# GNN layer with residual norm on one core: rows of x held in runs by partition, and an earlier order of the first loads

## The chip, the cores and the metric

One core of a Trainium2 chip runs the whole program. The metric is the device time of one execution in microseconds. It is 1736.49 us before the change, the median of three runs (1736.48 to 1737.98).

## The reference

`x` has 12500 nodes of 128 values, and there are 400000 edges, sorted by their destination. Each edge has one of two types.

```python
Xs = X[src]
m_data = Xs @ W_data.T + b_data
m_ctrl = Xs @ W_control.T + b_control
msg = jnp.where((edge_types == 0)[:, None], m_data, m_ctrl)
agg = jax.ops.segment_sum(msg, dst, num_segments=X.shape[0])
out = agg + (X @ W_self.T + b_self)
x = _layernorm(x + jax.nn.relu(out), axis=-1)
```

The sum over edges is done on rows of x, and the weights are applied once to the sums of each type.

## The kernel before

The 3125 chunks of 128 edges form 25 groups of 125 chunks (`NG`, `GC`). A group has four or five sets; there are 107 in all (`pairs`). A group's chunks are treated in two ways.

Most chunks of a set (20, "e") are *picked*: x lies in SBUF as `x3`, each fp32 value split into three bf16 parts, and a 0/1 matrix (`pick`, 128 x 100 cells x 32 ranks) lets TensorE choose the rows (`rows`, L899, tile `got`). ScalarE evicts the result (`emsg`, L907), and TensorE adds it into `sums` with a second 0/1 matrix over the nodes (`esel`, the node columns, made on VectorE by `select`). For this every edge of the set is given a cell and a rank in its cell: `give_slots` (L566) makes `O`, counts with `ltri` on TensorE, and forms `rank`, `rm`, `rv`; `put` and `spread` bring that through a small tile `there` in DRAM to all partitions as `pick`. A cell belongs to a *place*: x3 has 98 places (`NBLK`) of up to 128 rows. The index of a row is cut into its lane (partition) and its place in `prep(...).then` (L492).

The other chunks ("p") and the few edges without a slot (`spare_rows`, L862) are *gathered*: GpSimd's indirect DMA reads rows of `rows3`, a copy of x3 in DRAM with 768 bytes a row (`fetch`, L788). Gathered chunks enter from the third set on (`LAG = 2`). A first gather has to wait until rows3 is whole.

Sums are added to a running tile `acc` at places that are read from the chip's own table `place_i` (`place_of`, L772; `accumulate`, L778): VectorE's sequencer loads the place into a register for each addition. `finish` multiplies by the weights and normalises.

Before the first set, `split_x` (L268) brings x from DRAM in pieces of 14 blocks. In a block, row `b*128 + p` lies on partition p, so one piece's load consists of 14 runs of 512 bytes on each partition, issued by ScalarE's queue. `split` takes the three parts out of each piece with three ScalarE instructions (L286, L288) and two on VectorE (L290, L293), and `store` writes the piece to rows3 from SP's queue, in runs of 768 bytes. Four tiles `xt` hold pieces in flight. Meanwhile group 0 is prepared (`prep(0)`), the slots of sets 0 and 1 are given, and the small transfers run: `load(0)`, `load_first` (ten transfers of 25 numbers), weights and biases (nine). The order of instructions on each engine follows the code, but a scheduler may move an instruction within it; `tc.issue_after(i)` holds instructions until i is issued in that order. Each queue works strictly in its order.

Of the kernel before, what the change touches and what calls it, by code (L numbers as in the profile page):

```python
# [8 lines left out]
FP = mybir.dt.float32  # L9
# [35 lines left out]
NBLK = -(-N // P)  # L45
NQ = 25
# [4 lines left out]
AHEAD = 14  # L51
FAR = -(-PW // DPC)
# [102 lines left out]
def row_tables(nc, keep, tmp):  # L155
# [21 lines left out]
    nc.vector.tensor_single_scalar(pick_first, pick_first_cols(nc, tmp, col), 0.0, op=OP.is_equal)  # L177
# [16 lines left out]
def pick_first_cols(nc, tmp, col):  # L194

    cols = tmp.tile([P, 3, GC], FP, name="cols")
# [6 lines left out]
    return cols  # L203


def short_path(ctx, tc, const, ident, eps, wT, brow, bad, x, src, dst, etype, ws, bs, out):
# [52 lines left out]
    load_first("e")  # L259
    load_first("p")  # L260

    early, pro = ExitStack(), ExitStack()
    parted = []
# [4 lines left out]
    def split_x(pool):  # L268

        tiles, units = {}, []  # L270
        pieces = [(b, min(step, NBLK - b), P) for b in range(0, NBLK, step)]
        b, m, _ = pieces.pop()
        pieces += [(b, m - 1, P), (b + m - 1, 1, N - (NBLK - 1) * P)]

        def at(t, b, m, rows):
            return t[b * P:b * P + (m - 1) * P + rows, :].rearrange("(k p) d -> p k d", p=rows)

        def fetch(b, m, rows):
            t = tiles[b] = pool.tile([P, step, D], FP, name="xt")[:rows, :m, :]
            nc.scalar.dma_start(out=t, in_=at(x, b, m, rows))  # L280

        def split(b, m, rows):
            t = tiles.pop(b)
            part = x3[:rows, b:b + m]
            byte = t.bitcast(U8).rearrange("p k (d b) -> p k d b", b=4)
            nc.scalar.copy(part[:, :, 0, :], t.bitcast(BF).rearrange("p k (d b) -> p k d b", b=2)[:, :, :, 1])  # L286
            for j in range(2):
                nc.scalar.activation(part[:, :, 2 - j, :], byte[:, :, :, j], AF.Copy, scale=2.0 ** (8 * j - 23))  # L288
            power = pool.tile([P, step, D], BF, name="power", bufs=2)[:rows, :m, :]
            nc.vector.tensor_single_scalar(  # L290
                power.bitcast(I16), part[:, :, 0, :].bitcast(I16), -128, op=OP.bitwise_and
            )
            parted.append(nc.vector.tensor_tensor(  # L293
                part[:, :, 1:, :], part[:, :, 1:, :],
                power.rearrange("p k (j d) -> p k j d", j=1).to_broadcast([rows, m, 2, D]), op=OP.mult,
            ))

        def store():
            for b, m, rows in pieces:
                nc.sync.dma_start(  # L300
                    out=at(rows3, b, m, rows), in_=x3[:rows, b:b + m].rearrange("p k j d -> p k (j d)")
                )

        ahead = 4
# [9 lines left out]
        return units, store  # L314

    split_units, store_rows = split_x(pro.enter_context(tc.tile_pool(name="pro", bufs=4)))
# [4 lines left out]
    for i, (w, b) in enumerate(zip(ws, bs)):  # L321
        nc.sync.dma_start(out=wn[:, i, :], in_=w)
        row = b.rearrange("(o d) -> o d", o=1)
        nc.sync.dma_start(out=brow[:, i, :], in_=row)
        at = (0, CAP, 2)[i]
        nc.sync.dma_start(out=bias[at:at + 1, :], in_=row)
# [32 lines left out]
    for t in blks:  # L359
        nc.vector.memset(t, -1.0)  # L360
# [4 lines left out]
    for t in om_all:  # L365
        nc.vector.memset(t, 0.0)

    ltri = keep.tile([P, 4, P], BF, name="ltri")
    free, own = iota([4, P], [[P // 4, 4], [1, P]], 0, 0, "i6"), iota([4], [[P // 4, 4]], 0, 1, "i7")
# [4 lines left out]
    for a in range(4):  # L374
        tables = nc.vector.tensor_scalar(ltri[:, a, :], free[:, a, :], own_f[:, a:a + 1], None, op0=OP.is_gt)
# [5 lines left out]
    nc.vector.memset(worst, 0.0)  # L381
    over_n = keep.tile([P, len(each_e)], BF, name="over_n")

    bounds_of, from_of, pick_first = row_tables(nc, keep, tmp)
    least = tmp.tile([1, NG, NWIN], FP, name="least")
    for i, (_, _, c, _) in enumerate(windows(0)):
        nc.vector.memset(least[:, :, i:i + 1], float(max(0, c * DPC - PAD)))
    nc.vector.memset(x3[:, NBLK - 1], 0.0)
# [67 lines left out]
    def prep(g):  # L456
# [12 lines left out]
        def begin():  # L469
            nc.scalar.copy(sf, s)  # L470
# [21 lines left out]
        def then():  # L492
            parts = pre.tile([P, 2, GC], I32, name="parts")
            nc.vector.tensor_single_scalar(parts[:, 0, :], idx, 7, op=OP.logical_shift_right)
            nc.vector.tensor_single_scalar(parts[:, 1, :], idx, 127, op=OP.bitwise_and)
            code_e = vals2.rearrange("p n v t -> p v t n")[:, 1, 0]
            pk = pre.tile([P, GC], FP, name="pk", bufs=3)
            nc.vector.scalar_tensor_tensor(pk, idx, 256.0, code_e, op0=OP.mult, op1=OP.add)
# [67 lines left out]
    def give_slots(w):  # L566
# [5 lines left out]
        def behind():  # L572
            return tc.issue_after(placed[0].ins) if w > 1 else ExitStack()

        def block_matrix():
            O = s["held"] = two.tile([P, EC * NCELL], BF, name="O")
            s["O"] = O.rearrange("p (c j) -> p c j", j=NCELL)
            select(s["O"], cell_cols[w % 2], blk2)
# [140 lines left out]
    def pick_matrix(w):  # L719

        def half(a, b):
            t = slots[w]["pick"][:, a:b].rearrange("p j r -> p (j r)")
            with tc.issue_after(placed[0].ins):
                nc.vector.tensor_scalar(t, t, lane_f, None, op0=OP.is_equal)  # L724
# [3 lines left out]
    acc, added, parts_in = {}, [], {}  # L728
# [43 lines left out]
    def place_of(g, i):  # L772

        parts_in[g] = parts_in.get(g, 0) + 1
        with tc.issue_after(added[-2].ins) if len(added) > 1 else ExitStack():
            return nc.vector.value_load(raw["place"][0:1, g, i:i + 1], min_val=0, max_val=R - WMAX)  # L776
# [85 lines left out]
    def spare_rows(w):  # L862
# [3 lines left out]
        if n == P:  # L866
# [3 lines left out]
            in_offset=bass.IndirectOffsetOnAxis(ap=slots[w]["idx"][:n], axis=0),  # L870
        )

    def picked(w, tiled, ending, before):
# [8 lines left out]
        def choose(q0, n):  # L882

            sel = select(sp.tile([P, 10, 2 * EW], BF, name="esel")[:, :n], code_col, slots[w]["code"][:, q0:q0 + n])
# [220 lines left out]
    sp = ctx.enter_context(tc.tile_pool(name="sel", bufs=2))  # L1105
    fp = ctx.enter_context(tc.tile_pool(name="fin", bufs=2))
    merged(pick_matrix(0))
# [32 lines left out]
    for w in range(pairs):  # L1140
# [8 lines left out]
        if i == 3 and g + 2 < NG:  # L1149
            load(g + 2)  # L1150
# [173 lines left out]
```

## Time and profile before

| | |
|---|---|
| time, median of three | 1736.49 us |
| profiled execution, its own time | 1736.82 us |
| its span | 1735.1 us |
| granted TensorE clock | 0.998 |
| HBM read, written | 230.17 MB, 17.67 MB |
| first gather of `both` | 73.17 us |

Times are in microseconds from the start of the span. In a row of the timeline stand the start, the duration, the engine, the line, the instruction with output <- input and shapes, the count, and in brackets the idle time before it and what ended it. "SPq", "ACTq" and "DVEq" are what an engine's sequencer does itself, issues of DMAs and loads of registers among it. In the table of stretches stand the length, then for PE, PEld, DVE, ACT and POOL the busy time with the number of instructions, then the granted clock, the mean busy share of the 16 DMA engines and the GB/s moved. The share is summed over packets, which overlap a little, so that it can pass 1. In the groups stand busy time, mean of one in ns, then the idle time before them and what ended it.

### The profile page before, as it was taken

To read this page: it belongs to the slowest core of one execution; us is meant where nothing else is said; L and a number is where in the kernel's file an instruction comes from. 1 tells how busy PE (TensorE), PEld (TensorE's weight loads), DVE (VectorE), ACT (ScalarE), POOL (GpSimd) and SP (SyncE) were. 2 spreads that over 40 slices of the span, in tenths; PEclk is the share of its full clock that TensorE was granted. 3 is DMA by queue.
4 is the path that set the end of the run, shared out by engine and by line. 5 is a ranking of instruction groups with operands and counts; after the bars stand their busy time and mean duration, and the time that the engine had idled before them with its cause. 6 is when DMAs were issued, how large, how long until landed. Compare 5 with 4: busy or idle time off the path is not lost.

```text
span 1735.1 us, 67976 instructions
## 1 busy us (share of the span) xinstructions
PE 1585.6 (91%) x28250; PEld 1249.1 (72%) x28250; DVE 1559.6 (90%) x3642; ACT 1228.9 (71%) x2201; POOL 1243.4 (72%) x1059
## 2 busy tenths in 40 slices
PE   1699999999999999999999999999999999999997
PEld 0477777777677777777777777777777777777776
DVE  7898999999999999999898999899999898999983
ACT  5777777767777676767677777776777676777675
POOL 1276778877778776767787777776777777777671
PEclk9999999999999999999999999999999999999999
DMA  7844454555454454444545444544454544444441
GB/s 221 275 135 137 130 155 127 159 153 149 124 158 130 139 159 147 134 144 135 151 125 169 138 149 130 159 130 154 139 162 124 161 129 146 146 154 126 136 134 46
DMA packets 145646, 252.35 MB, mean 145 GB/s; under 512 B 35563, under 2 KB 111936, under 8 KB 145328
## 3 DMA queue, kind: packets, MB, share of 16 engines
q1 hardware_dynamic: 82670, 138.54, 23.6%
q0 software_dynamic: 50032, 102.98, 22.3%
q10 hardware_dynamic: 12626, 6.40, 1.3%
q8 instruction: 223, 3.65, 0.9%
q14 instruction: 95, 0.78, 0.1%
HBM read 230.17 MB, written 17.67 MB: 143 GB/s over the span
## 4 chain that ended last, share of the span: by engine, by line
DVE 43%; PE 39%; issue 9%; ACT 5%; DVEq 2%; DMA 2%; SPq 0%; ACTq 0%
PE sums L738 17%; PE got L893 13%; DVE esel L516 5%; DVE prod L622 4%; DVE pick L724 3%; DVE prod L617 3%; PE side L1012 3%; DVE rv L657 3%; DVE found L624 2%; DVE psel L516 2%; DVE prod L595 2%; DVE acc L782 2%; ACT emsg L907 2%; DVE O L516 2%; DVEq L776 2%
## 5 line engine op out<-in xcount | busy, mean ns | idle before, releaser
L793 POOL DMA_INDIRECT msg<-rows,idx_g x985 | 1174.3, 1192 | 361.6 <-issue 128.6
L907 ACT CAST emsg<-got 128x768 bf16<-128x768 f32 (+1 forms) x1070 | 953.7, 931 | 360.1 <-PE got L893 338.4
L738 PE MATMUL sums<-esel,emsg 128*128 128x176 bf16 x7704 | 686.6, 240 | 0.6 <-ACT emsg L907 0.4
L738 PEld LDWEIGHTS <-emsg 128*128 128x128 bf16 x7704 | 566.0, 98 | 102.8 <-issue 95.5
L893 PE MATMUL got<-x,pick 128*32 128x384 bf16 x10486 | 584.8, 330 | 15.2 <-DVE pick L724 9.7
L893 PEld LDWEIGHTS <-pick 128*32 128x32 bf16 x10486 | 239.7, 96 | 135.0 <-DVE pick L724 12.1
L516 DVE TENSOR_TENSOR esel<-code_col,code 128x1760 bf16<-128x1760 bf16 x321 | 293.0, 913 | 16.2 <-PE sums L738 14.9
L738 PE MATMUL sums<-psel,msg 128*128 128x48 bf16 x2955 | 183.6, 184 | 31.3 <-DVE acc L782 29.3
L738 PEld LDWEIGHTS <-msg 128*128 128x128 bf16 x2955 | 153.8, 97 | 62.4 <-issue 58.3
L622 DVE TENSOR_TENSOR prod<-prod 128x1200 bf16<-128x1200 bf16 x214 | 133.7, 625 | 4.7
L516 DVE TENSOR_TENSOR O<-cell_col,blk 128x2000 bf16<-128x2000 bf16 x107 | 127.6, 1193 | 8.2 <-ACT blk L420 3.7
L617 DVE TENSOR_TENSOR prod<-O,ahead 128x2000 bf16<-128x2000 bf16 x107 | 128.4, 1200 | 5.8 <-DVE ahead L613 3.5
L782 DVE TENSOR_TENSOR acc<-acc,sums 128x80 f32 (+3 forms) x357 | 98.9, 280 | 32.4 <-PE sums L738 29.8
L516 DVE TENSOR_TENSOR psel<-near_col,near 128x1200 bf16<-128x1200 bf16 x125 | 97.4, 779 | 23.1 <-issue 22.4
L724 DVE TENSOR_SCALAR pick<-pick,lane_f 128x3200 bf16<-128x3200 bf16 x107 | 112.8, 1054 | 0.6 <-DMA pick<-there 0.6
L868 POOL DMA_INDIRECT both<-rows,idx x54 | 63.4, 1174 | 64.6 <-ACT emsg L907 27.0
L669 PE MATMUL side<-rv,O 128*128 128x64 bf16 x2140 | 83.6, 195 | 23.0 <-DVE rv L657 21.5
L669 PEld LDWEIGHTS <-O 128*128 128x128 bf16 x2140 | 78.8, 100 | 24.9 <-DVE rv L657 21.8
L657 DVE TENSOR_TENSOR rv<-rm,vals 128x1280 bf16<-128x1280 bf16 x107 | 87.8, 820 | 0.0
L624 DVE TENSOR_REDUCE found<-prod 128x20 f32<-128x600 bf16 x107 | 83.0, 776 | 5.2 <-DVE prod L622 2.7
L595 DVE TENSOR_TENSOR prod<-O 128x1000 bf16<-128x1000 bf16 x107 | 71.8, 671 | 0.0
L605 PEld LDWEIGHTS <-ltri 128*128 128x128 bf16 x1284 | 40.4, 97 | 36.3 <-issue 34.5
(171 smaller groups left out, 1536.2 us busy)
## 6 DMA issues: line engine op xcount, KB each, us to landing
pick<-there SPq DMA_DIRECT2D x106, 800.0 KB
acc<-acc_start SPq DMA_DIRECT2D x23, 960.0 KB
msg<-rows,idx_g POOLq DMA_INDIRECT x985
rows<-x SPq DMA_DIRECT2D x6, 1344.0 KB
xs<-in_x_dram SPq DMA_DIRECT2D x99, 62.5 KB
out_dram<-h SPq DMA_DIRECT2D x99, 62.5 KB
xt<-in_x_dram ACTq DMA_DIRECT2D x6, 896.0 KB
there<-cell SPq DMA_DIRECT2D x106, 6.2 KB
```

Of the source, the lines that this page charges most:

```text
L516: nc.vector.tensor_tensor(sel.rearrange("p n (w t) -> p n w t", t=2), col[:rows].rearrange("p (o w t) -> p o w t", o=1, t=2).to_broadcast( ...
L617: nc.vector.tensor_tensor(prod[:, :, :NCELL], s["O"], ahead.rearrange("p (o j) -> p o j", o=1).to_broadcast([P, EC, NCELL]), op=OP.mult,)
L622: nc.vector.tensor_add(prod[:, :, :h], prod[:, :, :h], prod[:, :, h:2 * h])
L624: nc.vector.tensor_reduce(found, prod[:, :, :h], AX.X, OP.add)
L657: placed[:] = [nc.vector.tensor_tensor(rv.rearrange("p c v (r t) -> p c v r t", t=2), rm.rearrange("p c (o r t) -> p c o r t", o=1, t=2).t ...
L669: nc.tensor.matmul(s["rk"][:m, :2 * CAP], s["held"][:, c * NCELL:c * NCELL + m], s["rv"][:, c].rearrange("p v r -> p (v r)"), start=(c == ...
L724: nc.vector.tensor_scalar(t, t, lane_f, None, op0=OP.is_equal)
L738: last = nc.tensor.matmul(out, msg[:, j * D:(j + 1) * D], sel, start=(start and j == 0), stop=stop, skip_group_check=True)
L782: added.append(nc.vector.tensor_add(win, win, ps[:, :n * wide].rearrange("p (a w) -> p a w", w=wide)[:, :, :width]))
L793: return nc.gpsimd.indirect_dma_start(out=msg, out_offset=None, in_=rows3[:, :], in_offset=bass.IndirectOffsetOnAxis(ap=codes["p", g][0][: ...
L893: last = nc.tensor.matmul(ps[CAP * a:CAP * (a + 1), :], slots[w]["pick"][:, a * NQ + q, :], x3[:, 4 * q + a - a0].rearrange("p j d -> p (j ...
L907: s["out"] = nc.scalar.copy(msg[:, :n], ps[:, :n, :3 * D])
```

## The change

Partition p now holds the rows `98 p` to `98 p + 97`, so row n lies on lane n // 98 at place n % 98. Partition 127 has only 54 rows (`FULL`). x is loaded in eight pieces, named here p0 to p7: 14, 13, 14 and 13 places over 128 partitions, then 14, 14, 14 and 2 places over 127. On a partition, a piece is one run in DRAM. The first two loads are issued by ScalarE's queue, all others by SP's; the loads of p0 to p3 come ahead of `load_first`, the weights and the biases. The index loads of group 1 and `load_near` come after the stores of rows3.

```diff
+FULL = N - (P - 1) * NBLK
+LATE = 68
...
-        pieces = [(b, min(step, NBLK - b), P) for b in range(0, NBLK, step)]
-        b, m, _ = pieces.pop()
-        pieces += [(b, m - 1, P), (b + m - 1, 1, N - (NBLK - 1) * P)]
+        halves = [FULL // 2, FULL - FULL // 2]
+        sizes = [(n, P) for h in halves for n in (h - h // 2, h // 2)]
+        rest = NBLK - FULL
+        sizes += [(n, P - 1) for n in (step, step, step, rest - 3 * step)]
+        pieces, b = [], 0
+        for m, rows in sizes:
+            pieces.append((b, m, rows))
+            b += m
...
         def at(t, b, m, rows):
-            return t[b * P:b * P + (m - 1) * P + rows, :].rearrange("(k p) d -> p k d", p=rows)
+            c = t.shape[-1]
+            return bass.AP(tensor=t.tensor, offset=t.offset + b * c, ap=[[NBLK * c, rows], [c, m], [1, c]])
...
-        for p in pieces[:ahead]:
-            fetch(*p)
+        for k, p in enumerate(pieces[:ahead]):
+            fetch(*p, nc.sync if k > 1 else nc.scalar)
         for k, p in enumerate(pieces):
             def unit(k=k, p=p):
-                with tc.issue_after(ready.ins):
-                    split(*p)
+                split(*p)
                 if k + ahead < len(pieces):
-                    fetch(*pieces[k + ahead])
+                    fetch(*pieces[k + ahead], nc.sync)
```

In `split`, the first two ScalarE instructions of p0 come after the first instruction of `prep(0)` and all others after its last; VectorE's part comes after set 0's ranks, from place 68 on after set 0's pick. The cut of the index takes three VectorE instructions in place of two.

```diff
-            nc.vector.tensor_single_scalar(parts[:, 0, :], idx, 7, op=OP.logical_shift_right)
-            nc.vector.tensor_single_scalar(parts[:, 1, :], idx, 127, op=OP.bitwise_and)
+            lane, place = parts[:, 1, :], pre.tile([P, GC], FP, name="lane", bufs=1)
+            nc.vector.tensor_scalar(
+                place, idx, 0.5 * (1 - NBLK), 1.0 / NBLK, op0=OP.add, op1=OP.mult
+            )
+            nc.vector.tensor_scalar(lane, place, 2.0 ** 23, -2.0 ** 23, op0=OP.add, op1=OP.add)
+            nc.vector.scalar_tensor_tensor(parts[:, 0, :], lane, float(-NBLK), idx, op0=OP.mult, op1=OP.add)
```

The ten places of a group are loaded into registers by one instruction, at the group's first addition, without the check of their range in the program.

```diff
-            return nc.vector.value_load(raw["place"][0:1, g, i:i + 1], min_val=0, max_val=R - WMAX)
+        if g not in at_places:
+            with tc.issue_after(added[-2].ins) if len(added) > 1 else ExitStack():
+                _, at_places[g] = nc.values_load_multi_w_load_instructions(
+                    raw["place"][0:1, g, :], engines=[nc.vector.engine], min_val=0, max_val=R - WMAX,
...
+        return at_places[g][i]
```

In the prologue set 0's slots are given in one go, ahead of the splits, and set 0's first 19 node columns are made there too.

```diff
-        ready = [u() for u in prep(0)][-1]
-    split_units.pop(0)()
-    merged([(1.5, lambda: places_after(parted[2]))], evenly(all_slots(0) + all_slots(1)), evenly(split_units))
+        leading, *_, ready = [u() for u in prep(0)]
+    for u in all_slots(0):
+        u()
+    first_placed = placed[0]
+    first_pick, = [u() for _, u in pick_matrix(0)]
+    for q0, n in ((0, 10), (10, 9)):
+        made[0, q0] = node_columns(0, q0, n)
+    merged(
+        [(1.5, lambda: places_after(parted[2]))],
+        evenly(split_units, 0.0, 0.8),
+        evenly(all_slots(1), 0.45, 1.1),
+    )
...
-    store_rows()
+    stored = store_rows()
     spare_rows(0)
-    with tc.issue_after(placed[0].ins):
+    with tc.issue_after(stored.ins):
         load(1)
         load_near()
```

Beside these: the memsets of `blks`, `om_all`, `worst` and of x3's unused rows go from VectorE to GpSimd; `pick_first` is built in place, without a copy; `ltri`'s table of indices is 224 wide in place of 512; slot work of set 1 is held behind set 0's ranks; and the gather of spare rows has a bound on its indices (`bounds_check=N - 1`).

More of the change, by code (lines that the diff above doesn't have):

```diff
@@ L289, in split @@
[L289 to L296, printed above, removed]
+                with tc.issue_after((ready if b or j else leading).ins):
+                    nc.scalar.activation(part[:, :, 2 - j, :], byte[:, :, :, j], AF.Copy, scale=2.0 ** (8 * j - 23))
@@ L320, in short_path @@
     nc.gpsimd.memset(bias, 0.0)
[L321 to L326, printed above, removed]
+    with tc.issue_after(fetches[-1].ins):
+        load_first("e")
+        load_first("p")
+        for i, (w, b) in enumerate(zip(ws, bs)):
+            nc.sync.dma_start(out=wn[:, i, :], in_=w)
+            row = b.rearrange("(o d) -> o d", o=1)
+            nc.sync.dma_start(out=brow[:, i, :], in_=row)
+            at = (0, CAP, 2)[i]
+            nc.sync.dma_start(out=bias[at:at + 1, :], in_=row)
     def iota(shape, pattern, base, mult, name):
@@ L882, in choose @@
         def choose(q0, n):
-            sel = select(sp.tile([P, 10, 2 * EW], BF, name="esel")[:, :n], code_col, slots[w]["code"][:, q0:q0 + n])
+            sel = made.pop((w, q0), None) or node_columns(w, q0, n)
             for k in range(n):
@@ L1149, in short_path @@
         if i == 3 and g + 2 < NG:
-            load(g + 2)
+            with tc.issue_after(stored.ins):
+                load(g + 2)
         tiled, begin = {}, []
```

72 lines of the change are left out of this document (42 added, 30 removed).

## The prediction

> **What bounds the kernel now.** First the page: the shares of the engines and the chain that ended last.
>
> ```profile
> span 1735.1 us, 67976 instructions
> PE 1585.6 (91%) x28250; PEld 1249.1 (72%) x28250; DVE 1559.6 (90%) x3642; ACT 1228.9 (71%) x2201; POOL 1243.4 (72%) x1059
> DVE 43%; PE 39%; issue 9%; ACT 5%; DVEq 2%; DMA 2%; SPq 0%; ACTq 0%
> ```
>
> VectorE and TensorE share the chain, so the steady part has no single bound. Then the stretches, for where the two are not full.
>
> ```profile
> 0.00:20.00 20.00, 1.86 (x7) 1.41 (x7) 11.00 (x89) 1.68 (x3) 3.96 (x18) 1.00 0.72 210
> 40.00:60.00 20.00, 3.88 (x56) 2.47 (x56) 16.62 (x28) 14.98 (x12) 1.72 (x2) 1.00 1.02 338
> 60.00:80.00 20.00, 16.96 (x218) 11.96 (x222) 17.11 (x39) 15.59 (x31) 5.44 (x5) 1.00 0.76 226
> 100.00:400.00 300.00, 283.77 (x5143) 224.97 (x5141) 275.74 (x626) 215.78 (x383) 230.73 (x194) 1.00 0.47 140
> ```
>
> The columns are PE, PEld, DVE, ACT, POOL, granted clock, DMA share, GB/s. From 100 us on, PE is busy 95% and DVE 92%; until 60 us PE has almost nothing, and the DMA engines are full. So there are two places: a prologue of some 75 us, and the steady part. What ends the prologue is read from the order of time.
>
> ```profile
> 15.98 0.25 SPq L326 DMA_DIRECT2D bias<-in_L_gnn_b_self_dram  x1
> 65.15 1.24 SPq L300 DMA_DIRECT2D rows<-x  x1
> 73.17 1.04 POOL L868 DMA_INDIRECT both<-rows,idx  x1 [25.29 <-DMA xs<-in_x_dram]
> 76.04 0.17 DVE L444 CAST first<-first_all 125x25 f32<-125x25 int32 x1
> 78.66 1.04 DVE L724 TENSOR_SCALAR pick<-pick,lane_f 128x3200 bf16<-128x3200 bf16 x1
> 80.38 2.52 ACT L907 CAST emsg<-got 128x768 bf16<-128x768 f32 x3 [0.33 <-PE got L893]
> ```
>
> The last part of the table rows3 is issued at 65.15, the first gather from it goes at 73.17, set 1's pick is made at 78.66, and set 1's first eviction is at 80.38. From there the kernel repeats itself.
>
> **The change, part by part.** I call its eight pieces of x p0 to p7: 14, 13, 14, 13 places of 128 rows, then 14, 14, 14, 2 places of 127 rows. The decisive question is what a transfer over 127 partitions costs; none is in the trace. The nearest rows are transfers over 125.
>
> ```profile
> 4.00:6.00 2.00, 0.00 (x0) 0.00 (x0) 1.97 (x18) 0.00 (x0) 0.60 (x1) 1.00 1.14 342
> 374.00:375.00 1.00, 1.00 (x30) 0.79 (x30) 1.00 (x2) 1.00 (x2) 0.69 (x2) 1.00 0.36 109
> 1628.00:1630.00 2.00, 2.00 (x50) 1.66 (x48) 2.00 (x14) 1.58 (x4) 1.70 (x2) 1.00 0.93 388
> 372.42 1.53 SPq L1045 DMA_DIRECT2D out_dram<-h  x4
> out_dram<-h SPq DMA_DIRECT2D x99, 62.5 KB
> acc<-acc_start SPq DMA_DIRECT2D x23, 960.0 KB
> ```
>
> At 4 to 6 us the 128-row loads of x, in runs of 512 B, move 342 GB/s at a share of 1.14. At 374 us four stores of 125 rows, also in 512 B runs and issued within 1.53 us, move 109 GB/s at 0.36. Both ratios are 0.32, and 5/16 is 0.31: 125 rows ran on five engines, and four such transfers in flight used the same five. Five is the largest number up to 16 that divides 125. 127 is a prime, so the same reading gives one engine, the same for all eight such transfers. The other end is sixteen engines, as for 128 rows. I take one.
>
> The rate of one engine with long runs: at 1628 to 1630 (a load of 7.5 KB runs, 960 KB over 128) it is 388/(16 x 0.93) = 26.1 GB/s. The slow end is the mean of the SP queue, 138.54 MB at 23.6% of sixteen engines over the span, 21.1 GB/s.
>
> ```profile
> q1 hardware_dynamic: 82670, 138.54, 23.6%
> 79.57 0.28 SPq L680 DMA_DIRECT2D there<-cell  x1
> 83.50 0.34 SPq L682 DMA_DIRECT2D pick<-there  x1
> 19.56 0.34 SPq L439 DMA_DIRECT2D first_all<-in_dst_dram  x1
> 20.00 4.43 SPq L245 DMA_DIRECT2D srcs<-in_src_dram  x1
> 35.85 1.68 ACT L286 COPY x<-xt 128x1792 bf16<-128x1792 bf16 x1
> 37.43 3.29 ACT L288 ACTIVATE x<-xt 128x1792 bf16<-128x1792 uint8 x2
> 34.09 2.01 DVE L293 TENSOR_TENSOR x<-x,power 128x3584 bf16<-128x3584 bf16 x1
> ```
>
> The Trainium skill, DMA: Bandwidth & Descriptors, section "Why a DMA increments its semaphore by 16 and not by 1", says that a transfer is spread over the largest number of engines up to 16 that divides the slowest dimension on both sides, and names 127 partitions as ending on one. By that rule the five engines of the 125-row stores agree with the trace, and the sum is the one below; by the reading that any near-full tile sprays over all engines it would be the first rival.
>
> The sum on that one engine, in the order of SP's issues:
> - p4's load is SP's 23rd transfer, behind three index loads, two loads of x and the 19 small ones that end at 16.23 now. I start it at 17 (13 to 21).
> - Loads p4 to p6: 127 x 14 x 512 B each, p7 2 places: 2.86 MB, 110 us at 26.1.
> - This engine's share of the stores of p0 to p3: 8 rows x 54 x 768 B = 0.33 MB, 13 us.
> - Stores of p4 to p7: 127 x 44 x 768 B = 4.29 MB, 165 us. Each needs its piece split, 5.0 us on ScalarE (1.68 + 3.29) and 2.0 and a smaller mask on VectorE; all of that lies under the next transfer of 35 us or more.
> - Its share of set 1's pick, between the last two stores: 8 x 6.4 KB, 2 us.
> So rows3 ends leaving SBUF at 17 + 290 = 307. Behind it in the same queue are now the index loads of group 1 and first_all, since load(1) and load_near come after the stores: first_all takes some 5 us (issued at 19.56; the next issue frees at 24.43). The three index loads add 25 rows each on five engines, 2 us, and landing some 2 of the 3.9 between there's issue and pick's. VectorE's queue has `first` ahead of set 1's pick, so it waits until 316; behind it stand that pick, the ranks of set 2 and all placements. From `first` to set 1's first eviction is 4.3 us now (76.04 to 80.38): 320 in place of 80.4, later by 240.
>
> What is hidden under that: set 0 finishes early. Its pick needs only p0 to p3 on VectorE, but ScalarE's queue has the splits of p4 to p7 ahead of the first eviction, so set 0's evictions start near 135, and its 16 us (the span over 107 sets) are over before 160. Set 0's undivided ranks, the two node columns ahead, the memsets moved to POOL and the x loads ahead of the small ones all gain inside these idle 240 us, and so gain nothing. A clear backlog at set 1 may give back 3 us.
>
> The steady part:
>
> ```profile
> L776 DVEq TENSOR_LOAD <-place_i x232: 296/304/1402, 42.1 to 1721.3; - x116
> L776 DVEq FUSED_REGOPS  x232: 183/190/206, 43.4 to 1721.7; - x116
> L516 DVE TENSOR_TENSOR psel<-near_col,near 128x1200 bf16<-128x1200 bf16 x125 | 97.4, 779 | 23.1 <-issue 22.4
> L495 DVE TENSOR_SCALAR parts<-idx_g 128x125 int32<-128x125 int32 x25 | 6.0, 242 | 0.2 <-issue 0.2
> L498 DVE SCALAR_TENSOR_TENSOR pk<-idx_g,vals 128x125 f32<-128x125 int32 x25 | 7.0, 280 | 0.0
> ```
>
> 232 loads of a place, 0.5 us each on VectorE's sequencer, become 25 loads of ten registers. What of the old ones shows is the 22.4 us ahead of psel; VectorE has 43% of the chain, so 10 to 22 are worth having, and I take 13. A load of ten is not in the trace: between 0.30 us (as one) and 3.0 (as ten), 25 times, 8 to 75 us of sequencer; a fifth shows by the old ratio (22.4 of 232 x 0.5), so 2 to 15, and I take 5, nearer the row of one instruction. The split of an index into lane and place has three instructions for two: one more of 0.24 to 0.28 us, 25 times, 6 to 7, of which 43% is 3. The check of bounds on 54 gathers lies on POOL, busy 72%; it costs nothing while POOL waits for its paces. Together -5 (bounds -20 and +12).
>
> The Trainium skill, Runtime: NRT & Kernel Launch, section "Instruction fetch mechanics", gives about 200 ns a register even in bulk; by it a load of ten would be an estimated 2 us and the term 10 in place of 5, and no run here shows it.
>
> Sum against the profiled execution: 1735.1 + 240 - 3 - 5 = 1967 of span, and its own time was 1736.8, 0.3 above the median of 1736.49: 1968 us.
>
> **The rivals.**
> ```profile
> DVE parts L494 <- ACT idx_g L488: 7.8, 1, 7.8
> DVE x L293 <- issue: 2.5, 1, 2.5
> 0.81 13.81 ACTq L280 DMA_DIRECT2D xt<-in_x_dram  x4
> 41.12 5.53 DMA there<-cell
> 46.95 8.70 DMA pick<-there
> ```
>
> - Sixteen engines take 127 rows as they take 128 (faster). Then the prologue is short: ScalarE's first cast no longer stands behind four loads' issue (13.81 us), and VectorE's waits of 7.8 and 2.5 go; its queue meets set 0's pick early and stalls there some 2. For it: one DMA of 127 rows is built like one of 128. Against it: the 109 GB/s. Prologue -8, steady -5: 1723.
> - One engine each, but each transfer on the next engine (slower, less so). Loads land at 17 to 24 + 35, stores take 52 us side by side after 8 of split: rows3 is whole near 119 in place of 73, 46 later, and the steady part gives 5 back: 1777. Against it: four 125-row stores kept to 109 GB/s.
> - Sixteen engines and no gain: `there` and pick of set 0 (5.53 and 8.70 us of the chain) meet the loads and stores of x in flight and take as much longer as they start earlier; VectorE stands before that pick with the pieces from p2 on behind it, and the loads of ten places at their dear end take the steady gain: 1736.
>
> **How the numbers follow.** One shared engine 0.83, sixteen with a gain 0.11, engines in turn 0.04, no gain 0.02. The likeliest is 1968. At 21.1 GB/s the 290 become 359 and the time 2037; an earlier start (-4) and the best steady part (-15) give 1949, and 5% more rate 1935. The range is 1915 to 2040, which holds nearly all of the first case and leaves out the others. 0.2% (3.5 us) is about what a measurement of this kernel can tell from no change: faster 0.11, same 0.02, slower 0.87.
>
> **What would show it.** Right: DMA share near 0.06 and some 26 GB/s over most of 50 to 300 us, SP's last rows store far past 200, PE idle between about 160 and 315, the first gather past 300, and set 1's first eviction near 320. Wrong: xt loads of 127 rows landing within 5 us of their issue, share near 1 until 60 us, a first gather before 75. The steady part is right if VectorE's idle ahead of psel falls from 22 to a few us and PE's share between the first gather and the end stays at 94 to 96%.

## The result, and the profile after

| | before | after |
|---|---|---|
| time, median | 1736.95 us (4 runs, 1736.48 to 1737.98) | 2007.69 us (4 runs, 2005.87 to 2008.24) |
| span of the profiled execution | 1735.1 us | 2006.5 us |
| ratio | | 1.1557, 95% interval 1.1542 to 1.1573 |

The change costs 271 us. The page's shares and slices of the kernel after show where to look (each digit is a fortieth of the span, about 50 us):

```profile
span 2006.5 us, 67387 instructions
PE 1605.3 (80%) x28250; PEld 1254.1 (63%) x28250; DVE 1579.2 (79%) x3660; ACT 1231.7 (61%) x2201; POOL 1275.0 (64%) x1066
PE   0002004999999999999999999999999999999997
DVE  9212004999999998899899989989999889899893
DMA  2121014344444444444454444444444444544442
```

TensorE has the same 28250 matmuls and 20 us more busy time; what it lost are the first six slices, and there the DMA engines are nearly idle too, not full as they were before. This is SyncE's queue in the timeline (start, duration of the issues, what is moved):

```profile
30.75 53.03 SPq L285 DMA_DIRECT2D xt<-in_x_dram  x3
83.87 34.47 SPq L308 DMA_DIRECT2D rows<-x  x1
118.43 2.13 SPq L285 DMA_DIRECT2D xt<-in_x_dram  x1
120.65 56.47 SPq L308 DMA_DIRECT2D rows<-x  x5
177.21 50.69 SPq L696 DMA_DIRECT2D there<-cell  x1
227.99 6.32 SPq L308 DMA_DIRECT2D rows<-x  x1
259.44 21.31 SPq L698 DMA_DIRECT2D pick<-there  x1
280.85 3.15 SPq L308 DMA_DIRECT2D rows<-x  x1
284.05 28.68 SPq L246 DMA_DIRECT2D srcs<-in_src_dram  x1
315.71 1.45 SPq L450 DMA_DIRECT2D first_all<-in_dst_dram  x1
```

`there` is 6 KB, and its issue, 0.28 us before, takes 50.69: it stands behind the transfers ahead of it in the queue. The stretches of time tell how fast those go (columns as in the prediction: PE, PEld, DVE, ACT, POOL, granted clock, DMA share, GB/s):

```profile
84.00:118.00 34.00, 0.00 (x0) 0.00 (x0) 3.33 (x5) 4.87 (x3) 0.00 (x0) 1.00 0.06 26
120.00:122.00 2.00, 0.00 (x0) 0.00 (x0) 0.00 (x0) 0.00 (x0) 0.00 (x0) 1.00 1.03 428
179.00:227.00 48.00, 0.00 (x0) 0.00 (x0) 0.00 (x0) 0.00 (x0) 0.00 (x0) 0.50 0.06 27
```

A share of 0.06 is one engine of sixteen (1/16 = 0.0625), at 26 to 27 GB/s. The row at 120 us is a store of 128 rows, let in between: share 1.03, 428 GB/s. The loads land one after the other, as the waits of ScalarE's first pass over each piece show, and the stage that follows waits for the last store and the index loads behind it:

```profile
70.61 1.68 ACT L292 COPY x<-xt 127x1792 bf16<-127x1792 bf16 x1 [25.56 <-DMA xt<-in_x_dram]
105.15 1.68 ACT L292 COPY x<-xt 127x1792 bf16<-127x1792 bf16 x1 [29.67 <-DMA xt<-in_x_dram]
139.74 1.68 ACT L292 COPY x<-xt 127x1792 bf16<-127x1792 bf16 x1 [29.73 <-DMA xt<-in_x_dram]
149.54 2.53 ACT L934 CAST emsg<-got 128x768 bf16<-128x768 f32 x3
320.67 1.09 POOL L889 DMA_INDIRECT both<-rows,idx  x1 [271.64 <-DMA srcs<-in_src_dram]
325.94 0.18 DVE L455 CAST first<-first_all 125x25 f32<-125x25 int32 x1 [156.46 <-DMA first_all<-in_dst_dram]
330.77 0.80 ACT L934 CAST emsg<-got 128x768 bf16<-128x768 f32 x1 [0.60 <-PE got L920]
```

A load of 127 x 14 x 512 B every 34.5 us is 26.4 GB/s. Set 0 is evicted from 149.54 on, and then everything stands until 320. Set 1's first eviction is at 330.77, later by 250.4 than the 80.38 of before. From there to the end of the span are 1675.7 us, and before the change 1654.7: the steady part lost another 21. Set k's pick falls behind little by little: by 250 us at set 1, 251 at set 20, 258 at set 50 and 271 at set 106. Here are the two parts as stretches, before and after:

```profile
80.38:1735.10 1654.72, 1560.67 (x27937) 1231.32 (x27925) 1495.48 (x3460) 1176.59 (x2138) 1232.01 (x1034) 1.00 0.47 141
```

```profile
330.77:2006.50 1675.73, 1579.65 (x27941) 1236.38 (x27933) 1498.00 (x3483) 1178.76 (x2139) 1244.74 (x1032) 0.99 0.46 139
1346.70:1350.10 3.40, 3.30 (x34) 2.85 (x23) 2.98 (x8) 1.78 (x3) 2.52 (x3) 0.50 0.56 167
```

TensorE's idle time (the length less its busy time) is 94 us before and 96 after; what grew, by 19 us, is its busy time for the same matmuls. A small part of that is the granted clock: it falls to 0.50 for 3.4 us at 1346.7, 1612.9 and 1882.6 us, while the kernel before has 1.00 until 1728.6, 7 us from its end. By their length these three cost at most some 5 us, an estimate.

Two groups changed in that steady part. First the loads of ten, from the view of their tile (shortest, median and longest in ns), and two groups of the page, all of the kernel after; then the additions in the page of the kernel before (psel's row of before stands in the prediction):

```profile
L793 DVEq TENSOR_LOAD <-place_i x25: 1061/2294/2705, 328.2 to 1930.8; - x25
```

```profile
L531 DVE TENSOR_TENSOR psel<-near_col,near 128x1200 bf16<-128x1200 bf16 x125 | 96.2, 770 | 0.0
L803 DVE TENSOR_TENSOR acc<-acc,sums 128x80 f32 (+3 forms) x357 | 99.5, 280 | 72.5 <-PE sums L754 49.8
```

```profile
L782 DVE TENSOR_TENSOR acc<-acc,sums 128x80 f32 (+3 forms) x357 | 98.9, 280 | 32.4 <-PE sums L738 29.8
```

VectorE's idle time ahead of psel went from 22.4 us to none, and the idle time ahead of its additions rose by 40.1: the load of ten places stands right ahead of them. Its median of 2.29 us hides two kinds. After the first one, loads of 2.29 to 2.33 us and of 1.06 to 1.08 us take turns, and all 25 together are 43 us. Half of the 40.1 us ends with TensorE's sums (29.8 before, 49.8 after), so not all of it is the loads themselves.

One more thing is new. The new layout leaves 44 places of the last partition empty, so the memset that clears x3's unused rows grew. In the kernel before it was a short one on VectorE:

```profile
3.75 0.22 DVE L388 MEMSET x<- 128x192 uint32 x1
```

Now GpSimd clears these places on 32 partitions, and beside it a pair of short VectorE instructions takes as long (this pair took 0.91 us in the run with 112 and 15 rows, where it came before the memset):

```profile
6.26 14.34 POOL L399 MEMSET x<- 32x16896 bf16 x1
6.46 15.20 DVE L379 TENSOR_SCALAR i<-i 128x224 int32<-128x224 int32 x2
29.04 1.69 ACT L295 ACTIVATE x<-xt 128x1792 bf16<-128x1792 uint8 x1
31.23 1.20 DVE L531 TENSOR_TENSOR O<-cell_col,blk 128x2000 bf16<-128x2000 bf16 x1 [0.75 <-ACT blk L431]
```

Set 0's block matrix O starts at 31.23 us (21.41 before). p0's last pass on ScalarE, held behind the last instruction of `prep(0)`, ends at 30.73; only then is its buffer free, and p4's load goes at 30.75.

### The profile page after: what moved, and what is told of

The parts are those of the page before. It is cut to its first block, busy times and chain, and to the rows that moved or that the text cites. A ratio compares the mean times of both kernels' runs of the same rounds, so it can differ in the third digit from the quotient of the medians.

```text
span 2006.5 us, 67387 instructions
## 1 busy us (share of the span) xinstructions
PE 1605.3 (80%) x28250; PEld 1254.1 (63%) x28250; DVE 1579.2 (79%) x3660; ACT 1231.7 (61%) x2201; POOL 1275.0 (64%) x1066
## 3 DMA queue, kind: packets, MB, share of 16 engines
q1 hardware_dynamic: 71932, 143.17, 21.1%
## 4 chain that ended last, share of the span: by engine, by line
PE 37%; DVE 34%; issue 6%; ACT 4%; DMA 1%; DVEq 1%; POOL 1%; ACTq 0%; POOLq 0%; SPq 0%
PE sums L754 17%; PE got L920 12%; DVE esel L531 4%; PE side L1039 3%; DVE prod L638 3%; DVE pick L740 3%; DVE rv L673 3%; DVE found L640 2%; DVE prod L633 2%; DVE acc L803 2%; DVE psel L531 2%; DVE prod L611 2%; ACT emsg L934 2%; PE side L621 1%; DVE rm L531 1%
## 5 line engine op out<-in xcount | busy, mean ns | idle before, releaser
L754 PE MATMUL sums<-esel,emsg 128*128 128x176 bf16 x7704 | 695.8, 240 | 3.6 <-DVE acc L803 2.8
L920 PE MATMUL got<-x,pick 128*32 128x384 bf16 x10486 | 590.9, 331 | 109.0 <-ACT emsg L934 93.3
L889 POOL DMA_INDIRECT both<-rows,idx x54 | 71.6, 1326 | 315.5 <-DMA srcs<-in_src_dram 271.6
L754 PE MATMUL sums<-psel,msg 128*128 128x48 bf16 x2955 | 184.3, 184 | 43.1 <-DVE acc L803 40.5
L803 DVE TENSOR_TENSOR acc<-acc,sums 128x80 f32 (+3 forms) x357 | 99.5, 280 | 72.5 <-PE sums L754 49.8
L754 PE MATMUL sums<-esel,last 128*128 128x176 bf16 x159 | 21.3, 241 | 158.9 <-ACT last L982 158.9
L754 PEld LDWEIGHTS <-last 128*128 128x128 bf16 x159 | 13.2, 99 | 159.5 <-ACT last L982 159.2
L481 ACT CAST sf<-srcs 125x128 f32<-125x128 int32 x25 | 7.6, 302 | 157.9 <-DMA srcs<-in_src_dram 155.9
```

The costliest lines, as they stand in the source:

```text
L754: last = nc.tensor.matmul(out, msg[:, j * D:(j + 1) * D], sel, start=(start and j == 0), stop=stop, skip_group_check=True)
L803: added.append(nc.vector.tensor_add(win, win, ps[:, :n * wide].rearrange("p (a w) -> p a w", w=wide)[:, :, :width]))
L889: return nc.gpsimd.indirect_dma_start(out=both[:n, :], out_offset=None, in_=rows3[:, :], in_offset=bass.IndirectOffsetOnAxis(ap=slots[w][" ...
L920: last = nc.tensor.matmul(ps[CAP * a:CAP * (a + 1), :], slots[w]["pick"][:, a * NQ + q, :], x3[:, 4 * q + a - a0].rearrange("p j d -> p (j ...
```

## The experiments

The experiments ran on three other chips, on which the kernel before takes 1998 to 2026 us in place of 1737, so only differences from the kernel before on the same chip are compared. The table names the chips A, B and C; the kernel before takes 2026, 1998 and 2023 us on them. A difference is the ratio less one, times before's median there, with the interval of the ratio; the medians alone give 57.8 us for the first run and 19.6 for the loads of ten, the numbers that later expectations use.

| kernel | chip | difference from before, us (95%) |
|---|---|---|
| the change again | B | +273 (262 to 285) |
| one place a load | A | +248 (242 to 254) |
| 127 rows as 124 and 3 | A | +84 (79 to 89) |
| 127 rows as 112 and 15 | A | +54 (47 to 61) |
| 112 and 15, one place a load | B | +28 (23 to 34) |
| the same without the memset | B | +24 (17 to 30) |
| the same, places unchecked | B | +10 (4 to 16) |
| without the memset, index loads early | B | +16 (10 to 22) |
| the same, places unchecked | B | +4 (-3 to 10) |
| the same, stores not behind `there` | C | 0 (-2 to 3) |
| before, and loads of ten | A | +21 (14 to 28) |
| before, places unchecked | B | -8 (-12 to -3) |

**How many engines a transfer gets.** Each transfer of 127 rows is cut in two along the partitions, loads and stores alike, with `cut` 112 in one kernel and 124 in the other:

```diff
+        def runs_of(rows):
+            return [(0, rows)] if rows == P else [(0, cut), (cut, rows)]
...
-            fetches.append(queue.dma_start(out=t, in_=at(x, b, m, rows)))
+            for a, z in runs_of(rows):
+                fetches.append(queue.dma_start(out=t[a:z], in_=at(x, b, m, rows)[a:z]))
...
-                last = nc.sync.dma_start(
-                    out=at(rows3[:, :], b, m, rows), in_=x3[:rows, b:b + m].rearrange("p k j d -> p k (j d)")
-                )
+                for a, z in runs_of(rows):
+                    last = nc.sync.dma_start(
+                        out=at(rows3[:, :], b, m, rows)[a:z],
+                        in_=x3[a:z, b:b + m].rearrange("p k j d -> p k (j d)"),
+                    )
```

> The changed kernel with each transfer of 127 rows cut into 112 and 15 rows, nothing else. Theory A (a transfer runs on the largest number of engines up to 16 that divides its rows): 112 rows take 16 engines and 15 rows 15, SP's last store of rows3 is out before 85 us in place of 284, set 1's first eviction is near 85 in place of 331, and the time is 1760 (1745 to 1775), the rest over the kernel before being the steady part's. Rival B (the wait comes from SP's queue or from the long runs as such, whatever the number of rows): within 30 of 2008.

> The changed kernel with each transfer of 127 rows cut into 124 and 3 rows. Theory A: four engines and three, so DMA share near 0.25 and some 105 GB/s while they run; loads 27 us and stores 41 in place of 110 and 165, set 1's first eviction near 135, time 1810 (1795 to 1830). If 127 were a special slow case and every other number of rows ran wide, the time would be that of the cut into 112 and 15, within 10 us.

Stretches of the first kernel, then of the second, in which the DMA engines carry almost nothing but cut transfers (stores in the first; loads, then stores in the second):

```profile
78.00:82.00 4.00, 3.63 (x55) 2.36 (x55) 4.00 (x7) 3.94 (x6) 0.00 (x0) 1.00 1.02 393
```

```profile
30.00:38.00 8.00, 0.61 (x12) 0.52 (x12) 6.97 (x13) 8.00 (x6) 0.00 (x0) 1.00 0.25 75
80.00:88.00 8.00, 4.84 (x68) 3.21 (x66) 7.91 (x17) 6.73 (x11) 0.00 (x0) 0.96 0.26 108
```

112 rows, with the 15 rows beside them, take all sixteen engines (share 1.02), 124 rows four (0.25 and 0.26). Largest divisors up to 16: 16 for 112, 4 for 124, and before 5 for 125 and now 1 for 127. That the rows are few or nearly full makes no difference. The first gather, at 320.67 us in the changed kernel, goes at 88.79 with 112 and 15 rows and at 129.84 with 124 and 3. The losses left are larger than theory A had (54 in place of 23, 84 in place of 73), so something else costs as well.

**The loads of ten.** One place a load again, in the changed kernel; and the loads of ten alone, in the kernel before:

```diff
-        if g not in at_places:
-            with tc.issue_after(added[-2].ins) if len(added) > 1 else ExitStack():
-                _, at_places[g] = nc.values_load_multi_w_load_instructions(
...
-        return at_places[g][i]
+        with tc.issue_after(added[-2].ins) if len(added) > 1 else ExitStack():
+            return nc.vector.value_load(raw["place"][0:1, g, i:i + 1], min_val=0, max_val=R - WMAX)
```

> The changed kernel with one place loaded at a time, as before. After set 1's first eviction the changed kernel takes 1675.7 us where the kernel before took 1654.7. Theory C (the loads of ten places, 2.3 us each on VectorE's sequencer, make the steady part slower): 1988 (1983 to 1993). Rival D (the steady part is slower by something else: the third instruction of the index cut, the bounded gathers, TensorE's clock after the long idle stretch): 2003 to 2012.

> The kernel before with the loads of ten places alone. Theory C: 1757 (1750 to 1763), VectorE idle ahead of acc, not of psel. Rival D: the loads of ten gain what was forecast of them, 1725 to 1737.

Alone they cost 21 us, as theory C said, and taken out of the change they give back about as much (273 less 248, on two chips). Their row in the kernel before with loads of ten:

```profile
L777 DVEq TENSOR_LOAD <-place_i x25: 1062/1319/2307, 80.8 to 1957.7; - x25
```

Here too, after the first one, loads of 2.3 and of 1.06 us take turns, 42 us in all: 1.7 us on average, between five and six times the 0.30 of one place.

**The change on the experiments' chip.** The kernel as it is:

> The changed kernel as it is, for its distance from the kernel before on the chip of these runs. If the parts add up (transfers of 127 rows 219 us, loads of ten 20, memset 5, order 24): 255 to 285 us over it. If the chip changes the size of a part: outside of that.

+273, where the first chip gave +271: the distance carries over, though all times there are 13 to 15% longer.

**Both suspects undone, and then the memset.** The cut of 112 and 15 with one place a load; and on top of it a DMA from a tile of zeros in place of the memset:

```diff
-    nc.gpsimd.memset(x3[P - CAP:, FULL:], 0.0)
+    nought = keep.tile([P, 2 * D], BF, name="nought")
+    nc.vector.memset(nought, 0.0)
+    nc.scalar.dma_start(
+        out=x3[P - 1:, FULL:].rearrange("p k j d -> p (k j d)").rearrange("p (r c) -> p r c", c=2 * D),
+        in_=nought[P - 1:, :].rearrange("p (r c) -> p r c", r=1).to_broadcast([1, (NBLK - FULL) * 3 // 2, 2 * D]),
+    )
```

> The changed kernel with each transfer of 127 rows cut into 112 and 15, and one place a load as before the change: both large suspects undone at once. Theory A (the parts add up: 57.8 us with the cut alone, 19.6 us of them the loads of ten): 38 us over the kernel before, and the first eviction of set 1's stage at 105 to 115 us in place of 80.4, since set 0's pick still stands at 50 to 54 us and its gathers start at 88 in place of 73. Rival B (with the transfers out of the way the loads of ten are hidden, and what is left is the new order alone): 55 us or more over it. Rival C (the new order gains once nothing stalls it): 0 or below.

> As the run before it, and GpSimd's memset of 32x16896 is taken away: the places of partition 127 that no load fills are cleared by a DMA from a small tile of zeros. Theory A (VectorE's 14 us stand still because GpSimd writes for 14 us beside it): the VectorE instruction of 14 us is gone, set 0's first block matrix O starts near 21 us in place of 29.6, and 8 to 12 us of the 38 go. Rival B (VectorE waited for something else at that place, or the stall is covered by the loads of x): O stays near 29, and the time within 3 us of the run before.

The first leaves 28, a little under theory A's 38. VectorE of the first, then VectorE and SyncE of the second:

```profile
6.47 15.20 DVE L385 TENSOR_SCALAR i<-i 128x224 int32<-128x224 int32 x2
55.36 1.05 DVE L746 TENSOR_SCALAR pick<-pick,lane_f 128x3200 bf16<-128x3200 bf16 x1 [5.45 <-DMA pick<-there]
```

```profile
15.70 1.20 DVE L542 TENSOR_TENSOR O<-cell_col,blk 128x2000 bf16<-128x2000 bf16 x1 [0.33 <-ACT blk L442]
20.00 12.21 SPq L289 DMA_DIRECT2D xt<-in_x_dram  x8
44.82 1.05 DVE L751 TENSOR_SCALAR pick<-pick,lane_f 128x3200 bf16<-128x3200 bf16 x1 [8.44 <-DMA pick<-there]
79.72 1.22 DVE L751 TENSOR_SCALAR pick<-pick,lane_f 128x3200 bf16<-128x3200 bf16 x1
104.16 0.17 DVE L466 CAST first<-first_all 125x25 f32<-125x25 int32 x1
119.70 1.05 DVE L751 TENSOR_SCALAR pick<-pick,lane_f 128x3200 bf16<-128x3200 bf16 x1
```

With the memset goes the VectorE instruction of 15.20 us: O starts at 15.70, p4's load at 20.00, and set 0's pick is copied 10.5 us sooner. The mechanism of theory A is there. Of the time only 5 us show (28 to 24), and the intervals overlap. O at 15.70 is also 5.7 us ahead of the kernel before, and set 0's pick 10.9 us (44.82 against 55.68); but set 2's pick is at 119.70, against 91.87 in the kernel before on the first chip and 99.12 in a kernel of the old order on this chip (next). Against that kernel on the same chip the new order is 11 us ahead at set 0 and 3 at set 1 (79.72 against 82.96), and 21 behind at set 2: it loses 24 us between set 1 and set 2.

**The check of the range.** Single loads without it, in the kernel before and in the changed order:

```diff
-            return nc.vector.value_load(raw["place"][0:1, g, i:i + 1], min_val=0, max_val=R - WMAX)
+            _, got = nc.values_load_multi_w_load_instructions(
+                raw["place"][0:1, g, i:i + 1], engines=[nc.vector.engine], min_val=0, max_val=R - WMAX,
...
+        return got[0]
```

> The kernel before with its single loads of a place, without the check of the range that each carries; nothing else. Theory A (the prediction's: what singles cost shows ahead of psel, 22.4 us of idle, and goes with the instructions of the sequencer): 5 to 13 us under the kernel before. Rival B (the load itself is the cost, and the check nothing): within 3 us of it.

> The changed kernel with the 112 and 15 row cut, no memset, and one place a load without its check: what is left is the new order of loads, ranks and columns. Theory A: the second run's time plus the difference that the third shows from the kernel before, so 15 to 30 us over it if the new order costs what it seemed to. Rival C (the new order is worth something once nothing stands in it): under the third run's time.

The kernel before gains 8 us by it, and is the one kernel here that beats both. Its loads still take 0.30 us, and what stood ahead of psel is gone all the same. Of this kernel, the tile of the places, the page and the timeline, and at last the group of psel in the changed order with single checked loads and no memset:

```profile
L776 DVEq TENSOR_LOAD <-place_i x232: 296/304/945, 82.4 to 1979.6; - x116
```

```profile
L516 DVE TENSOR_TENSOR psel<-near_col,near 128x1200 bf16<-128x1200 bf16 x125 | 96.9, 776 | 0.0
```

```profile
82.96 1.05 DVE L724 TENSOR_SCALAR pick<-pick,lane_f 128x3200 bf16<-128x3200 bf16 x1
99.12 1.05 DVE L724 TENSOR_SCALAR pick<-pick,lane_f 128x3200 bf16<-128x3200 bf16 x1
```

```profile
L542 DVE TENSOR_TENSOR psel<-near_col,near 128x1200 bf16<-128x1200 bf16 x125 | 97.2, 778 | 25.3 <-issue 25.1
```

So the idle time ahead of psel came of the check (one FUSED_REGOPS of 0.19 us and one assertion behind each load), not of the load. In the changed order leaving out the check gives 14 us (24 to 10), which ends a little below theory A's 15 to 30; rival C, less than the kernel before without the check, is not there.

**What the new order loses between set 1 and set 2.** In the run without the memset first_all's packets of four bytes run at 78 to 84 us, beside the first gathers (in the kernel before: 20 to 26, in the prologue). The times in the expectation, 86 to 94 and 32 to 36, are not those of these two kernels. One line lets these loads start as before:

```diff
-    with tc.issue_after(stored.ins):
+    with tc.issue_after(placed[0].ins):
         load(1)
         load_near()
```

> The run without the memset (112 and 15 rows, one place a load), and the index loads of set 1 and first_all's may again start once set 0's ranks are placed, as before the change, and not behind the last store of x. Theory A (what is left of the loss, about 24 us, comes of these loads: 3125 packets of four bytes ran at 86 to 94 us, beside the first gathers, in place of 32 to 36 us beside the loads of x): `first` at 80 to 90 us in place of 104, pick of set 2 at 95 to 105 in place of 120, and 12 to 24 us less, so 0 to 12 us over the kernel before. Rival B (TensorE was held there by something else, its granted clock of 0.5 to 0.7 among it, and `first` only stood behind it in VectorE's queue): within 5 us of the run without the memset, about 24 over the kernel before. Rival C (four-byte packets in the way of the loads of x): slower than that run.

> As the run before it, with the single loads of a place without the check of their range. Theory A: 5 to 10 us less than that run, so between 10 us under the kernel before and 7 over it. Rival C (the new order gains once nothing is in its way: set 0's pick is copied at 44.8 us in place of 55.7): 10 to 20 us under it.

`first` moves to 78.58 us, a little sooner than theory A has it, but set 2's pick only to 115.63, and the time to +16: 8 us less with overlapping intervals. The loads were not the larger part. Without the check it is +4, inside theory A's bounds for that run; rival C's 10 to 20 us under it are not there. Stretches of the kernel with early index loads, from set 1's pick on:

```profile
78.00:86.00 8.00, 5.66 (x67) 3.66 (x68) 4.73 (x11) 2.24 (x4) 5.03 (x4) 0.50 0.18 39
94.00:102.00 8.00, 2.23 (x21) 1.27 (x21) 2.56 (x10) 2.43 (x3) 4.52 (x5) 0.75 0.20 56
```

Nothing is full there: no engine, and the DMA at a fifth. VectorE's longest wait between the two picks, 7.69 us until 99.44, ends with what the profile calls "remote" and does not name further. The granted clock is 0.50 to 0.75. In the run without the memset it stands at 0.50 for 31 us between 79 and 124 us, in the old order without the check for 10. Whether that is a cause of the loss or comes of TensorE's waits was not tried. What was tried is what comes late. In SyncE's queue the last seven stores of x stood behind `there` of set 1, so in the kernel with early index loads and unchecked places the first gather went at 79.14 us, ahead of set 1's pick by less than 1 us (5.5 in the kernel before):

```diff
-            queue = nc.sync if w else nc.gpsimd
+            queue = nc.sync if w > 1 else nc.gpsimd
```

> As the run with the early index loads and single unchecked loads, and `there` and pick of set 1 go over GpSimd's queue as set 0's do, so that the last seven stores of x no longer stand behind `there` of set 1 in SyncE's queue (there it waited at 62 us, while the pieces of 127 rows were split by 53 to 61 us). Theory A (the first gathers come too late for set 1, 79 us in place of 73, with a lead of under 2 us over set 1's pick in place of 5.5, and TensorE then waits in order): the first gather at 68 to 73 us, the loss of some 17 us between set 1's pick and set 2's shrinks below 8, and the time is 8 to 18 us less than that run's, 5 to 15 under the kernel before. Rival B (the loss there has another cause): the gathers move and the time stays within 4 us of that run, at the kernel before or above it.

VectorE and GpSimd of this kernel:

```profile
71.11 1.27 POOL L899 DMA_INDIRECT both<-rows,idx  x1 [0.63 <-DVE ahead L640]
79.83 1.04 DVE L751 TENSOR_SCALAR pick<-pick,lane_f 128x3200 bf16<-128x3200 bf16 x1
103.23 1.05 DVE L751 TENSOR_SCALAR pick<-pick,lane_f 128x3200 bf16<-128x3200 bf16 x1
```

The gather goes 8 us sooner and set 2's pick 11 us (114.31 without this edit); from set 1 to set 2 are 23.4 us, where the old order takes 16.2 (82.96 to 99.12). That much of theory A holds. The time does not follow: the ratio to the kernel before is 1.0002 (0.9990 to 1.0015), in place of 1.0018 (0.9987 to 1.0049), so the 5 to 15 us under the kernel before are not there, and rival B's time is. The 11 us won at set 2's pick don't show at the end, and what takes them is open; the two runs are on two chips, C and B.

## Why the prediction was right, and where it was off

It said 1968 us (1915 to 2040) and slower; the median is 2007.7. By its steps:

- **One engine for 127 rows: right**, in the share (0.06), the rate (26 to 27 GB/s against 26.1) and the order of the queue, and by the cuts to sixteen and four engines. By the rule of the Trainium skill (DMA: Bandwidth & Descriptors, section "Why a DMA increments its semaphore by 16 and not by 1") 124 rows take four engines and 112 sixteen, and the traces agree (shares 0.25 and 1.02). The rivals with sixteen engines, or each transfer on the next, fall with the row at 84 to 118 us, where one engine carries everything.
- **The chain of transfers: 290 us, right within 3%.** At 26.4 to 27 GB/s it is 280 to 287, and the one engine is at work from 31 us to about 314.
- **Its start: off by 14 us**, the largest error of the stage. The step "I start it at 17 (13 to 21)" counted SyncE's issues (p4's load is the 25th there, not the 23rd, which changes nothing) and overlooked a buffer: four pieces are in flight, and p4 waits until ScalarE is through with p0, whose last pass is held behind the end of `prep(0)`, on VectorE. The prediction named the memsets moved to GpSimd as a gain that is hidden, and put no cost on them; in fact the one that clears x3 held VectorE for 15 us. p4's load is issued at 30.75 and lands at 70.61, 40 us later, where the next two take 34.5 each. Without the memset it is issued at 20.00, inside the prediction's bounds. With 14 late at the start, some 7 won on the chain and 3 lost behind it the stage comes out 10 late: `first` at 325.94 for 316, the first eviction at 330.77 for 320. +250 in place of +240.
- **What is hidden: right.** Set 0's evictions begin at 149.54 (135 predicted, again by the start) and the new order's early ranks and columns make no difference in the 156 us for which VectorE stands still; the memset, counted with them, shows in the start. A backlog of 3 given back is not seen.
- **The steady part: -5 predicted, +21 measured, outside its bounds (-20 to +12).** The sum's term for a load of ten (5 us, 2 to 15) was mis-sized. It took a fifth of the sequencer's time as visible because a fifth of the old loads' time showed, and a duration near one register's. Measured: the 25 loads take 43 us in the changed kernel and 42 in the kernel before with loads of ten. There they cost 21 us in all, although they also leave out the check, which by itself is worth 8. So they are worth some 29 us, an estimate across two chips: seven tenths of their time shows. Old loads lay spread among other work, while a load of ten stands in one block before an addition, and TensorE waits for those (its idle time ahead of the sums of gathered rows that ends with an addition went from 29.3 to 40.5 us). That this is how the time is lost is argued and not shown, since TensorE's idle time as a whole rose by 2 us only. The other half of that step, 13 us to win ahead of psel, was there as idle time (22.4 to 0), but it belongs to the check, which a single load can drop too: -8 alone. The Trainium skill's 200 ns a register (Runtime: NRT & Kernel Launch, section "Instruction fetch mechanics") makes an estimated 2 us of a load of ten; the rows have 1.7 on average in both kernels with loads of ten, so it was the better guide to the duration, not to the sign: with 2 us the prediction had 10 and would still have said no loss.
- Its test for the steady part did not tell: psel's idle time went to 0 and TensorE's share between 400 and 1900 us is 94.7% (281.0 to 286.0 us of each 300, 1419.85 of 1500), both as for "right", while the part became longer; from 400 to 1600 us of the kernel before it is 94.7% too. A busy share near the top is no evidence for a gain.
- That the total lies in the range is in part luck. The range's upper end, 2040, was made for an engine at 21.1 GB/s, which didn't come. At 26.1 the sum with its own worst start (+4) and worst steady part (+12 in place of -5) ends at 1989, below the 2007.7 measured.

Together: 1735.1 + 250.4 + 21.0 = 2006.5, the span. On the experiments' chips the parts are 219 us for 127 rows (248 less 28), 21 for the loads of ten, 5 for the memset and 24 for all that is left, the new order of the first loads among it: 269 of 273. The 219 is taken between two chips, and with the 5 and the 24 it adds up to 248 by how it is taken; what the sum tests is only that the 21 of the loads alone fit the 25 between 248 and 273. In the changed kernel itself, with the first gather 8 us ahead of set 1's pick, the loss of the new order does not appear as such: from set 1's pick to set 2's are 14.5 us there (328.78 to 343.27), 13.2 before. It lies under the wait, and only shows once the wait is taken away. Of the 24 the index loads may be 8, by overlapping intervals; what the rest comes of stays open. Nor was it tried whether the new order would do better on a chip like the first.

## What to carry to other kernels

Count the partitions of a transfer before its bytes: 128 rows went over sixteen engines, 127 over one, and one odd row in a layout turned a prologue of 75 us into 320; where a layout has it, cut the transfer at 112 and 15. (Even so no kernel of the new layout here was shown to beat the kernel before.) When an edit merges many small loads into one, ask where the one stands: a stall in one block ahead of an addition showed to an estimated seven tenths, while of the small pieces a fifth had shown. Follow a moved transfer's buffer, and not only its queue, back to what frees it.

## What the runs showed that was not expected

- While GpSimd ran one memset of 14.34 us, VectorE stood in a pair of instructions on 128x224 int32 for 15.20 us; in another run with the same memset three short instructions stood for 14 us, two scalar operations and an operation on two tensors between them. Three casts beside the smaller memsets ahead of it (0.6 to 1.6 us) took 3.1 to 3.2 us. Without the memset the 15.20 us are gone. The Trainium skill (SBUF — State Buffer, section "Who interferes with whom") has this as a lock: GpSimd and VectorE share a pair of ports, whichever issues first holds it for its whole instruction, and VectorE's copies, casts and scalar operations in their two-port modes wait. The rows of casts and scalar operations agree; the operation on two tensors is not of these forms, and may only have stood in line. The prediction had not asked the page when it put no cost on the memsets.
- One program takes 1737 us on one chip and 1998 to 2026 on three others. VectorE's instructions last the same there (prod of 2000 columns: 1200 ns on both), and TensorE's got goes from 330 to 335 ns, but the idle time ahead of it goes from 15.2 to 111.6 us (kernel before on the first chip, kernel before with loads of ten on another). The granted clock of the kernel before is 0.998 on the first chip and 0.968 to 0.985 on the others. What TensorE waits for there the profile doesn't show ("issue", or its own evictions); the differences between kernels were much the same, +271 and +273.
